# Transposing x by block loads and VectorE in place of TensorE, in a two-layer graph kernel

## The chip, the core and the metric

The kernel runs on one core of a Trainium2 chip. The core has a matrix engine (TensorE, PE in the profile), a vector engine (VectorE, DVE), a scalar engine (ScalarE, ACT), a general one (GpSimd, POOL) and a queue (SyncE, SP) that issues transfers to 16 DMA engines. Each engine works through its own queue in order; semaphores hold an instruction until what it needs is there. The metric is the time of one execution on the device in microseconds, as a median of several runs. All data is float32.

## The reference

x has 64 batches of 256 tokens with 512 features; `adj` is one 256 x 256 matrix of zeros and ones. Two layers follow each other, each with its input added and a layer norm after it:

```python
# layer 0: attention with 8 heads of 64, masked by adj
q, k, v = (x @ W + b for W, b in ((Wq, bq), (Wk, bk), (Wv, bv)))   # each 256 x 512 per batch
scores = q_h @ k_h.T / 8 + (1 - adj) * -1e9                         # per head
x = layernorm(x + (softmax(scores) @ v) @ Wo + bo)
# layer 1: graph attention with one pair of vectors a1, a2
h = x @ W
e = leaky_relu(s1[:, None] + s2[None, :], 0.2) * adj                # s1 = h @ a1, s2 = h @ a2
x = layernorm(x + elu(softmax(e) @ h + beta * h))
```

What matters here is `q`, `k` and `v`: TensorE sums over the partitions, so x must stand with its features on the partitions (x transposed, `xT`) before it can be multiplied by the weights. In memory it stands with tokens as rows.

## The kernel before

Work goes by pairs of batches. A pair has two halves, batch 0 and batch 1. The function `pair` makes `xT`, `qT`, `kT` and `V` for both; the function `batch` does the rest for each: scores and exponentials by keys (`scores`), their sums (`sums`) and reciprocals, the mix with V (`mix`), the output projection (`o`), the layer norm, the second layer's row and column terms (`logits`), its softmax and transpose (`attention`), its mix with x (`spread`), and the product with W (`u`), ending in `finish`.

`q`, `k`, `v`, `o`, `spread` and `u` are each done by `project` with seven block products in place of eight (Strassen's way, in Winograd's form), called `chain`, `cross`, `second`, `fourth` (or `pair`) after the PSUM tiles that they add into. The sums that this asks of the right side are made by GpSimd in `token_sums` (L393 to L412): `xS` from `xT`, `oS` from `oT`, `yS` from `yT`. The weights and sums of Wq and Wk are fetched anew for every pair, seven `piece` loads each (L386, L381), with six buffers.

Nothing is issued at once. `Plan.op` records an operation with its engine, an assumed duration, what it reads and what it writes; `Plan.place` then sets one order for all engines. TensorE's order is fixed by hand: `turn` gives each operation a pair (round, place in the round). `ROUND` (L23) is the order of the 20 stages in a round and `LATER` (L26) says how many rounds after the pair's number a stage runs, so that several pairs are in flight. Round r does `scores` and `v` of pair r, `q` and `k` of pair r + 1, `sums1` of pair r - 1, and so on. The other engines are filled around TensorE's order by due time, with limited buffers (`slots`); only TensorE's last 60 operations are placed by what is ready. The order that comes out is issued as it stands, so each engine's queue is fixed when the kernel is built. All transfers but a few at the start go through the one SP queue.

Around the change: x comes in twice. The second load (L673) is the residual, with tokens on the partitions. The first one (L600) feeds the transpose: four loads of 256 KB per pair into two buffers `xin`, whose rows are 2 KB each. TensorE transposes 128 x 128 blocks against an identity matrix into a PSUM tile `tr_x` (L593), four blocks per operation, 16 per pair, and ScalarE copies each PSUM tile into `xT` (L596). In a round the stage `x` stands behind `spread0` and is done for the next pair, which uses it in the same round at `q`.

Also near the change: after `sums`, VectorE takes the reciprocal `inv` (L741), SP stores it as `rows` (L752) and loads it back spread over partitions as `inv_all` (L756); VectorE then scales `oT` by it (L782), GpSimd makes `oS`, and `o` can run.

Of the kernel before, what the change touches and what calls it, by code (L numbers as in the profile page):

```python
# [16 lines left out]
P = 128  # L17
# [2 lines left out]
ALPHA = 0.2  # L20
NEG = -1000000000.0

ROUND = ("sums1", "mix1", "scores0", "v", "o1", "attention0", "u0", "spread0", "x", "logits1",  # L23
         "sums0", "mix0", "scores1", "q", "attention1", "o0", "spread1", "k", "logits0", "u1")

LATER = {"x": -1, "q": -1, "k": -1, "v": 0, "scores0": 0, "scores1": 0, "sums0": 0, "sums1": 1, "mix0": 0, "mix1": 1,  # L26
         "o0": 0, "o1": 1, "logits0": 0, "logits1": 1, "attention0": 1, "attention1": 1, "spread0": 1, "spread1": 1,
         "u0": 2, "u1": 1}
SAFE = 1e15


# [22 lines left out]
class Plan:  # L54
# [11 lines left out]
    SWITCH = 250.0  # L66
    LATER = 15000.0
    OPEN = 60
# [43 lines left out]
    def place(self):  # L112
# [21 lines left out]
        for n, o in enumerate(ops):  # L134
            if due[n] is None:
                due[n] = max((due[d] + (self.LATER if ops[d][0] == "PE" else ops[d][1]) for d in o[3]), default=0.0)

# [90 lines left out]
def gnn_two_layers(ctx: ExitStack, tc: tile.TileContext, x, adj, Wq, bq, Wk, bk, Wv, bv, Wo, bo, W, a, beta, out):  # L228
    nc = tc.nc
    B, N, D = x.shape  # L230
    NT = N // P
    C = D // P
# [6 lines left out]
    dram = ctx.enter_context(tc.tile_pool(name="dram", bufs=1, space=bass.MemoryType.DRAM))  # L239
# [14 lines left out]
    plan = Plan(slots)  # L254
    stay = []
    A = slice(None)

    def sb(tag, shape, name):
        return Buf(sb_pool, tag, [P] + shape, name)

    def ps(shape, name):
        return Buf(ps_pool, "ps", [P] + shape, name)
# [11 lines left out]
    def blk(t):  # L274
        return slice(t * P, (t + 1) * P)

    def half(i):
        return slice(i * F, (i + 1) * F)


    ident = const.tile([P, P], F32, name="ident")
# [4 lines left out]
    def load(w_sb, w):  # L286
        for c in range(C):
            plan.op("SP", 1000, lambda c=c: nc.sync.dma_start(w_sb[:, c], w[blk(c), :]), [], [(w_sb, c)])
# [40 lines left out]
    def transposed_mask():  # L329
        acc = ps([NT, N], "tr_adj")  # L330

        def pe():
            for k in range(NT):
                for t in range(NT):
                    nc.tensor.transpose(acc[:, k, blk(t)], adj_sb[:, t, blk(k)], ident)

        plan.op("PE", 430, pe, [adj_sb], [acc], claims=[maskT_sb])
        plan.op("DVE", 690, lambda: nc.vector.tensor_scalar(
            maskT_sb[A], acc[A], -1.0, -NEG * HD ** 0.5, ALU.add, ALU.mult), [acc], [maskT_sb])
# [53 lines left out]
    def token_sums(T, keys, name, width=P):  # L393

        S = sb("xS" if width == P else "xP", [3, 2, width], name)
        q = {(k, j): (lambda k=k, j=j: T[:, 2 * k:2 * k + 2, j * width:(j + 1) * width])
             for k in range(2) for j in range(2)}  # L400
        t2, t3, t4 = ((lambda i=i: S[:, i]) for i in range(3))

        def sub(dst, p, m, reads, writes):
            plan.op("POOL", 180 + 545 * width // P, lambda: nc.gpsimd.tensor_tensor(dst(), p(), m(), ALU.subtract),  # L404
                    reads, writes)

        sub(t3, q[1, 1], q[0, 1], keys(1, 1) + keys(0, 1), [(S, 1)])
        sub(q[0, 1], q[0, 1], q[0, 0], keys(0, 1) + keys(0, 0), keys(0, 1))
        sub(t2, q[1, 1], q[0, 1], keys(1, 1) + keys(0, 1), [(S, 0)])
        sub(t4, q[1, 0], t2, keys(1, 0) + [(S, 0)], [(S, 2)])  # L410
        return [(q[0, 0], keys(0, 0)), (q[1, 0], keys(1, 0)), (q[1, 1], keys(1, 1)), (t4, [(S, 2)]),
                (q[0, 1], keys(0, 1)), (t2, [(S, 0)]), (t3, [(S, 1)])]  # L412
# [51 lines left out]
    def gather(quarter, bias=None, wide=False):  # L464

        def copy(q, acc):
            (dst, key), (src, acc) = quarter(q), acc[::-1]
            if bias is None:
                plan.op("ACT", 590 if wide else 370, lambda: nc.scalar.copy(dst(), src()), [acc], [key])  # L469
                return  # L470
            for f in range(2):
                plan.op("ACT", 370, lambda f=f: nc.scalar.activation(
                    dst()[:, f, :], src()[:, f, :], AF.Identity,
                    bias=bias[:, 2 * q[0] + f:2 * q[0] + f + 1]), [acc], [key])

        def add(q, acc):
            (dst, key), (src, acc) = quarter(q), acc[::-1]
            plan.op("DVE", 690 if wide else 420, lambda: nc.vector.tensor_add(dst(), src(), dst()), [acc, key], [key])

        return copy, add  # L480
# [89 lines left out]
    def pair(m, at, general=False):  # L570

        def turn(what):

            plan.turn = ((m or 0) + LATER[what], ROUND.index(what))

        def dram(ap, s):
            return ap[at].rearrange("o (t p) d -> p o t d", p=P)[:, s]

        Xs = [sb("xin", [NT, D], f"xin_{m}_{s}") for s in range(2)]

        def tokens(s, t):
            return [(Xs[s], (t, 0)), (Xs[s], (t, 1))]


        xT, qT, kT = (sb("two", [C, 2 * N], f"{n}_{m}") for n in ("xT", "qT", "kT"))
        V = sb("two", [2 * NT, D], f"v_{m}")

        def tr_x(s, t):
            X, tr = Xs[s], ps([C, P], "tr_x")

            def pe():
                for c in range(C):
                    nc.tensor.transpose(tr[:, c, :], X[:, t, c * P:(c + 1) * P], ident)  # L593

            plan.op("PE", 430, pe, tokens(s, t), [tr], claims=[xT])
            plan.op("ACT", 680, lambda: nc.scalar.copy(xT[:, :, blk(2 * t + s)], tr[A]), [tr], [(xT, (t, s))])  # L596

        for s in range(2):
            for t in range(NT):
                plan.op("SP", 1400, lambda s=s, t=t: nc.sync.dma_start(Xs[s][:, t, :], dram(x, s)[:, t, :]), [],  # L600
                        tokens(s, t), first=m == 0 and s == 0 and t == 0)
        turn("x")
        for s in range(2):
            for t in range(NT):
                tr_x(s, t)

        right = token_sums(xT, lambda k, j: [(xT, (j, s)) for s in range(2)], "xS", N)

        def qk(left, bias, dst):
            project(left, right, True, [dst], *gather(  # L610
                lambda q: (lambda: dst[:, 2 * q[0]:2 * q[0] + 2, q[1] * N:(q[1] + 1) * N], (dst, q)), bias, True),
                width=N, raw=m == 0)

        if m == 0:
            wq_sb, wk_sb = sb("two", [C, D], "wq_sb"), sb("two", [C, D], "wk_sb")
            load(wq_sb, Wq)
            load(wk_sb, Wk)
            lq, left["q"] = streamed(wq_sb, Wq, "wq_sums")
            lk, left["k"] = streamed(wk_sb, Wk, "wk_sums")
            turn("q")  # L620
            qk(lq, bq_sb, qT)
            plan.turn = (plan.turn[0], plan.turn[1] + 0.5)
            transposed_mask()
            turn("k")
            qk(lk, bk_sb, kT)
            left["v"] = weight_sums(wv_sb, "sv_sb", "POOL")
            plan.turn = (0, ROUND.index("x"))
            left["o"] = residual_bias()
        else:
            turn("q")  # L630
            qk(left["q"], bq_sb, qT)
            turn("k")
            qk(left["k"], bk_sb, kT)
        turn("v")
        project(left["v"], right, False, [V], *gather(
            lambda q: (lambda: V[:, 2 * q[1]:2 * q[1] + 2, half(q[0])], (V, q)), wide=True), width=N)
        for s in range(2):
            batch(m, s, qT, kT, V, dram, general)

    def batch(m, s, qT, kT, V, dram, general):  # L640
# [5 lines left out]
        def turn(what):  # L646
            plan.turn = ((m or 0) + LATER[f"{what}{s}"], ROUND.index(f"{what}{s}"))

# [226 lines left out]
        if b == 0:  # L875
            plan.turn = (0, ROUND.index("k"))
            left["w"] = second_layer_constants()
# [123 lines left out]
    for m in range(B // 2):  # L1001
        pair(m, slice(2 * m, 2 * m + 2))
# [6 lines left out]
    def check():  # L1009
# [5 lines left out]
            claims=[least])  # L1015
# [9 lines left out]
    with tc.If(again != 0):  # L1025
# [3 lines left out]
        with tc.For_i(0, B, 2) as i:  # L1029
            for tile_ in stay:  # L1030
                tile_.parts = {}
            plan = Plan({**slots, "half": slots["half"] - 1})
# [33 lines left out]
```

## Time and profile before

| what | value |
|---|---|
| time, median of 3 runs (lowest to highest) | 2830.74 us (2830.37 to 2831.67) |
| span of the profiled execution | 2826.7 us |
| granted TensorE clock, mean | 0.997 |
| PE `tr_x`, L593 | 512 transposes, 63.1 us busy |
| ACT `xT`, L596 | 128 copies, 592 ns each in the median |
| loads of `xin`, L600 | 128 of 256 KB, 3.6 us from issue to landing |
| GpSimd `xS`, L404, idle ahead of it for ScalarE's `xT` | 87.8 us in 32 waits |
| HBM read and written | 220.73 MB and 36.17 MB |

How to read the profile: "busy" is the time in which an engine worked on an instruction; its share is of the span. PEld is TensorE's loading of the stationary operand, which runs beside its products. The chain of work that ended last is followed back from the last instruction, at each step to what released it, or to the instruction ahead of it on its engine. A group of instructions is a source line, an engine and the tiles written and read; "idle before" is time in which that engine had nothing to do just ahead of such an instruction, with the cause of most of it. One round is 86.75 us in the middle of the run.

### The profile page before, as it was taken

Reading aid. Unit: us, or ns where it says so; the run is one execution under the profiler, and the core shown is the slowest. Engines: PE = TensorE matmul, PEld = TensorE weight load, DVE = VectorE, ACT = ScalarE, POOL = GpSimd, SP = SyncE. Lnnn points to the kernel's source line nnn. Section 1 sums busy time; section 2 is a strip of 40 time slices with the busy share of each in tenths; the row PEclk is TensorE's granted clock in tenths of the full one; section 3 lists DMA queues with packets and bytes.
Section 4 is the critical chain, followed back from the end, with each engine's and each line's share of the span. In section 5 each row is a group of like instructions: output and inputs, shape, how many; then the busy total and the mean of one; then the engine's idle time right before and its main releaser. Section 6 shows DMA issues by size and latency. Waiting matters only on the chain.

```text
span 2826.7 us, 47456 instructions
## 1 busy us (share of the span) xinstructions
PE 2793.3 (99%) x16771; PEld 2367.1 (84%) x16771; DVE 2136.6 (76%) x4126; ACT 1319.3 (47%) x2875; POOL 1753.7 (62%) x2379
## 2 busy tenths in 40 slices
PE   9999999999999999999999999999999999999997
PEld 7788888888888888888888888888888888888875
DVE  6668777787877777777877777777778777787877
ACT  3345444454554444444544544445445444454544
POOL 5656765566655667556666556675566765566655
PEclk9999999999999999999999999999999999999999
DMA  6223322232222333323322223333233322232211
GB/s 231 75 75 106 98 86 76 86 113 90 91 91 79 101 98 98 94 67 95 113 90 87 81 81 113 90 98 95 71 98 105 97 87 75 87 112 90 75 44 41
DMA packets 181506, 260.07 MB, mean 92 GB/s; under 512 B 15256, under 2 KB 96400, under 8 KB 181264
## 3 DMA queue, kind: packets, MB, share of 16 engines
q1 hardware_dynamic: 181136, 256.95, 29.5%
q8 instruction: 137, 2.24, 0.3%
q14 instruction: 105, 0.86, 0.1%
q0 software_dynamic: 128, 0.01, 0.0%
HBM read 220.73 MB, written 36.17 MB: 91 GB/s over the span
## 4 chain that ended last, share of the span: by engine, by line
PE 97%; DVE 1%; POOL 0%; DMA 0%; ACT 0%; issue 0%; SPq 0%; DVEq 0%; POOLq 0%; ACTq 0%
PE ps_chain L433 32%; PE ps_cross L433 21%; PE ps_pair L433 10%; PE ps_sc L714 8%; PE ps_pv L691 8%; PE ps_fourth L433 6%; PE ps_second L433 6%; PE ps_den L737 2%; PE tr_x L593 2%; PE tr_a L929 1%; DVE junk L883 1%; PE tr_s L893 0%; PE ps_plain L497 0%; DVE junk L538 0%; DMA xin<-in_x_dram 0%
## 5 line engine op out<-in xcount | busy, mean ns | idle before, releaser
L725 POOL TENSOR_TENSOR both<-pT 128x256 f32<-128x256 f32 x512 | 368.5, 748 | 82.0 <-ACT pT L723 82.0
L723 ACT ACTIVATE pT<-pT 128x512 f32<-128x512 f32 x512 | 308.0, 630 | 123.2 <-DVE pT L721 122.0
L721 DVE TENSOR_TENSOR pT<-ps_sc,maskT_sb 128x512 f32<-128x512 f32 x512 | 316.2, 677 | 3.4 <-PE ps_sc L714 3.4
L883 DVE SCALAR_TENSOR_TENSOR junk<-x,wa_sb 128x512 f32<-128x512 f32 x256 | 246.4, 1015 | 0.7 <-ACT x L566 0.7
L714 PE MATMUL ps_sc<-qT,kT 64*128 64x256 f32 x2048 | 241.7, 384 | 2.6 <-DVE pT L721 2.6
L691 PE MATMUL ps_pv<-pT,v 128*64 128x256 f32 x2048 | 236.6, 384 | 0.0
L714 PEld LDWEIGHTS ps_sc<-qT,kT 64*128 64x128 f32 x2048 | 199.6, 187 | 43.6 <-issue 24.2
L560 POOL TENSOR_SCALAR rs<-mv 128x1 f32<-128x1 f32 x256 | 55.7, 218 | 286.5 <-DVE mv L557 284.2
L566 ACT ACTIVATE x<-x,nmr,rs 128x512 f32<-128x512 f32 x256 | 200.6, 811 | 48.3 <-DVE nmr L564 45.2
L911 POOL TENSOR_TENSOR e<-e,adj_sb 128x512 f32<-128x512 f32 (+1 forms) x65 | 91.5, 1408 | 205.9 <-DVE e L908 205.9
L691 PEld LDWEIGHTS ps_pv<-pT,v 128*64 128x64 f32 x2048 | 142.1, 137 | 91.8 <-issue 15.4
L969 POOL TENSOR_TENSOR att_sums<-attT 128x128 f32<-128x128 f32 x126 | 57.7, 458 | 203.0 <-ACT attT L933 191.7
L933 ACT COPY attT<-tr_a 128x512 f32<-128x512 f32 x64 | 37.5, 586 | 277.7 <-PE tr_a L929 277.6
L556 DVE BATCH_NORM_STATS2 bn<-x 128x6 f32<-128x512 f32 x256 | 164.5, 683 | 2.3
L675 POOL TENSOR_TENSOR x<-x,res_sb 128x512 f32<-128x512 f32 x128 | 161.0, 1279 | 2.2 <-issue 1.1
L561 POOL TENSOR_TENSOR rs<-rs,neg_half 128x1 f32<-128x1 f32 x256 | 145.4, 568 | 21.3
L564 DVE SCALAR_TENSOR_TENSOR nmr<-mv,rs 128x1 f32<-128x1 f32 x256 | 102.0, 408 | 72.5 <-POOL rs L561 72.1
L469 ACT COPY yT<-ps_chain 128x256 f32<-128x256 f32 x126 | 46.9, 373 | 231.4 <-PE ps_chain L433 225.2
L404 POOL TENSOR_TENSOR xS<-xT 128x512 f32<-128x512 f32 x64 | 87.4, 1366 | 90.3 <-ACT xT L596 87.8
L860 DVE TENSOR_TENSOR x<-x,ps_chain 128x256 f32<-128x256 f32 x252 | 100.2, 418 | 56.6 <-PE ps_chain L433 56.2
L969 POOL TENSOR_TENSOR X_sums<-x 128x256 f32<-128x256 f32 x126 | 120.4, 956 | 33.7 <-ACT x L566 33.7
L404 POOL TENSOR_TENSOR oS<-oT 128x256 f32<-128x256 f32 x126 | 92.5, 734 | 64.1 <-DVE oT L782 59.2
(232 smaller groups left out, 7482.9 us busy)
## 6 DMA issues: line engine op xcount, KB each, us to landing
xin<-in_x_dram SPq DMA_DIRECT2D x128, 256.0 KB, 3.6
x<-in_x_dram SPq DMA_DIRECT2D x64, 512.0 KB, 3.7
out_dram<-x SPq DMA_DIRECT2D x128, 256.0 KB, 3.1
inv_all<-rows SPq DMA_DIRECT2D x126, 256.0 KB, 3.8
wq_sums<-wq_sums SPq DMA_DIRECT2D x124, 256.0 KB, 2.6
wk_sums<-wk_sums SPq DMA_DIRECT2D x124, 256.0 KB, 2.8
wq_sums<-in_L_gnn_Wq_dram SPq DMA_DIRECT2D x93, 256.0 KB, 2.7
wk_sums<-in_L_gnn_Wk_dram SPq DMA_DIRECT2D x93, 256.0 KB, 2.8
```

The lines of the kernel that those rows point to most:

```text
L404: plan.op("POOL", 180 + 545 * width // P, lambda: nc.gpsimd.tensor_tensor(dst(), p(), m(), ALU.subtract), reads, writes)
L433: nc.tensor.matmul(dst[:, f, :], lhs, rhs, start=start and f == 0 and c == 0, stop=c == inner - 1, skip_group_check=True)
L556: plan.op("DVE", 690, lambda: nc.vector.bn_stats(bn[A], X[:, t, :]), [(X, (t, 0)), (X, (t, 1))], [bn])
L566: plan.op("ACT", 810, lambda: nc.scalar.activation(X[:, t, :], X[:, t, :], AF.Identity, bias=nm[A], scale=rs[A]), [nm, rs], [(X, (t, 0)), ...
L675: plan.op("POOL", 1270, lambda t=t: nc.gpsimd.tensor_tensor(X[:, t, :], X[:, t, :], res_sb[A], ALU.add), [res_sb], tokens(t))
L691: nc.tensor.matmul(acc[r * HD:(r + 1) * HD, i, :], V[:, 2 * k + s, h * HD:(h + 1) * HD], pT[h][:, k, :], start=k == 0, stop=k == NT - 1)
L714: nc.tensor.matmul(acc[j][:, k, :], kT[r:r + HD, c, key_blk(k)], own(qT, r, c), start=True, stop=True)
L721: plan.op("DVE", 690, lambda h=h, i=i: nc.vector.tensor_add(pT[h][A], acc[i][A], maskT_sb[A]), [acc[i], maskT_sb], [pT[h]])
L723: plan.op("ACT", 620, lambda h=h: nc.scalar.activation(pT[h][A], pT[h][A], AF.Exp, scale=1.0 / HD ** 0.5), [pT[h]], [pT[h]])
L725: plan.op("POOL", 725, lambda h=h, i=i: nc.gpsimd.tensor_tensor(both[c][:, i, :], pT[h][:, 0, :], pT[h][:, 1, :], ALU.add), [pT[h]], [(bot ...
L883: plan.op("DVE", 780, lambda t=t, i=i, junk=junk: nc.vector.scalar_tensor_tensor(junk[A], X[:, t, :], 1.0, wa_sb[:, i, :], op0=ALU.mult, o ...
L969: plan.op("POOL", ns, lambda: nc.gpsimd.tensor_tensor(dst(), p(), m(), op), reads, writes)
```

## The change

TensorE no longer transposes x. Each batch is loaded by four transfers, one for each group of 32 partitions `f`. A transfer puts 32 tokens on 32 partitions, and along each partition it lays runs of 32 features (128 bytes): partition `32 f + j` holds, for feature chunk `c` and token block `b`, the 32 features of token `32 b + j`. In that form every block of 32 tokens by 32 features lies on the right partitions and in the right columns, and only has to be transposed in itself. One VectorE instruction per batch does that for all 128 blocks and writes `xT` directly; PSUM and ScalarE are not used. An empty TensorE operation of the plan keeps the stage `x` a place in TensorE's order, which is where the buffer of `xT` is claimed.

The order of a round changes as well. `x` is done two rounds ahead in place of one (`LATER` -2), `u0` moves a round earlier and `u1` a round later, and `logits1`, `spread0`, `spread1`, `attention1`, `u0` and `u1` change places. The purpose is to take the transposes and their copies off TensorE and ScalarE, and to leave the loads and the transposes time ahead of `q`.

```diff
-ROUND = ("sums1", "mix1", "scores0", "v", "o1", "attention0", "u0", "spread0", "x", "logits1",
-         "sums0", "mix0", "scores1", "q", "attention1", "o0", "spread1", "k", "logits0", "u1")
+ROUND = ("sums1", "mix1", "scores0", "v", "o1", "attention0", "u1", "x", "spread0", "sums0", "mix0", "scores1", "q",
+         "logits1", "o0", "u0", "attention1", "k", "spread1", "logits0")
...
-LATER = {"x": -1, "q": -1, "k": -1, "v": 0, "scores0": 0, "scores1": 0, "sums0": 0, "sums1": 1, "mix0": 0, "mix1": 1,
+LATER = {"x": -2, "q": -1, "k": -1, "v": 0, "scores0": 0, "scores1": 0, "sums0": 0, "sums1": 1, "mix0": 0, "mix1": 1,
...
-         "u0": 2, "u1": 1}
+         "u0": 1, "u1": 2}
...
-        def tr_x(s, t):
-            X, tr = Xs[s], ps([C, P], "tr_x")
-
-            def pe():
-                for c in range(C):
-                    nc.tensor.transpose(tr[:, c, :], X[:, t, c * P:(c + 1) * P], ident)
-
-            plan.op("PE", 430, pe, tokens(s, t), [tr], claims=[xT])
-            plan.op("ACT", 680, lambda: nc.scalar.copy(xT[:, :, blk(2 * t + s)], tr[A]), [tr], [(xT, (t, s))])
-
+        def blocks(s):
+
+            xb = sb("xin", [C, N], f"xin_{m}_{s}")
+            rows = x[at].rearrange("o (b j) (c f i) -> o f j c b i", j=32, f=4, i=32)[s]
+            for f in range(4):
+                plan.op("SP", 700, lambda f=f: nc.sync.dma_start(
+                    xb[f * 32:(f + 1) * 32].rearrange("p c (b i) -> p c b i", i=32), rows[f]), [], [(xb, f)],
+                    first=m == 0 and s == 0 and f == 0)
+            plan.op("DVE", 1140, lambda: nc.vector.transpose(
+                xT[A].rearrange("p c (t s n) -> p c t s n", t=NT, s=2)[:, :, :, s, :],
+                xb[A].rearrange("p c (t n) -> p c t n", t=NT)), [xb, (xT, "turn")], [(xT, (t, s)) for t in range(NT)])
+
+
+        turn("x")
+        plan.op("PE", 0, lambda: None, [], [(xT, "turn")], claims=[xT])
         for s in range(2):
-            for t in range(NT):
-                plan.op("SP", 1400, lambda s=s, t=t: nc.sync.dma_start(Xs[s][:, t, :], dram(x, s)[:, t, :]), [],
-                        tokens(s, t), first=m == 0 and s == 0 and t == 0)
-        turn("x")
-        for s in range(2):
-            for t in range(NT):
-                tr_x(s, t)
+            blocks(s)
```

More of the change, by code (lines that the diff above doesn't have):

```diff
@@ L577, in dram @@
             return ap[at].rearrange("o (t p) d -> p o t d", p=P)[:, s]
-        Xs = [sb("xin", [NT, D], f"xin_{m}_{s}") for s in range(2)]
-        def tokens(s, t):
-            return [(Xs[s], (t, 0)), (Xs[s], (t, 1))]
         xT, qT, kT = (sb("two", [C, 2 * N], f"{n}_{m}") for n in ("xT", "qT", "kT"))
         V = sb("two", [2 * NT, D], f"v_{m}")
-        def tr_x(s, t):
-            X, tr = Xs[s], ps([C, P], "tr_x")
-            def pe():
-                for c in range(C):
-                    nc.tensor.transpose(tr[:, c, :], X[:, t, c * P:(c + 1) * P], ident)
-            plan.op("PE", 430, pe, tokens(s, t), [tr], claims=[xT])
-            plan.op("ACT", 680, lambda: nc.scalar.copy(xT[:, :, blk(2 * t + s)], tr[A]), [tr], [(xT, (t, s))])
-        for s in range(2):
-            for t in range(NT):
-                plan.op("SP", 1400, lambda s=s, t=t: nc.sync.dma_start(Xs[s][:, t, :], dram(x, s)[:, t, :]), [],
-                        tokens(s, t), first=m == 0 and s == 0 and t == 0)
-        turn("x")
-        for s in range(2):
-            for t in range(NT):
-                tr_x(s, t)
+        def blocks(s):
[10 more added lines that the diff above has]
+        plan.op("PE", 0, lambda: None, [], [(xT, "turn")], claims=[xT])
+        for s in range(2):
+            blocks(s)
         right = token_sums(xT, lambda k, j: [(xT, (j, s)) for s in range(2)], "xS", N)
```

## The prediction

> **What bounds the kernel now.** I read the page first: busy shares, then the chain that ended last.
>
> ```profile
> span 2826.7 us, 47456 instructions
> PE 2793.3 (99%) x16771; PEld 2367.1 (84%) x16771; DVE 2136.6 (76%) x4126; ACT 1319.3 (47%) x2875; POOL 1753.7 (62%) x2379
> PE 97%; DVE 1%; POOL 0%; DMA 0%; ACT 0%; issue 0%; SPq 0%; DVEq 0%; POOLq 0%; ACTq 0%
> ```
>
> PE is busy for 99% of the span and is 97% of the chain. A busy PE need not be a full one, so the next view is the table by stretches, for one round (two batches) in the middle, beside the first and the last stretch (columns: stretch, length, busy PE, PEld, DVE, ACT, POOL, clock, DMA share, GB/s).
>
> ```profile
> 0.00:88.00 88.00, 81.16 (x433) 68.04 (x434) 53.63 (x83) 31.41 (x64) 54.76 (x63) 1.00 0.61 204
> 1290.00:1376.75 86.75, 86.75 (x526) 73.82 (x525) 66.24 (x129) 41.25 (x90) 54.40 (x75) 1.00 0.30 92
> 2740.00:2827.00 87.00, 64.80 (x343) 49.62 (x339) 68.18 (x152) 35.67 (x75) 46.45 (x70) 0.92 0.14 47
> ```
>
> A round in the middle has no idle PE at all: 86.75 of 86.75 us, at full clock. So its length is the sum of what stands in PE's queue, and a matmul removed there shortens it by its place in the queue, as long as no wait opens. VectorE has 20.5 us free in a round, ScalarE 45, GpSimd 32, and the DMA engines 70%. How much the transposes hold is read in the timeline of PE (start, length, line, names), from their start to the next group's:
>
> ```profile
> 1346.89 0.61 PE L433 MATMUL ps_chain<-att_sums,X_sums 128*128 128x128 f32 x4
> 1347.34 1.91 PE L593 MATMUL tr_x<-ident,xin 128*128 128x128 f32 x16
> 1349.09 0.38 PE L893 MATMUL tr_s<-ident,s 128*128 128x128 f32 x2
> ```
>
> 16 transposes hold PE from 1347.34 to 1349.09: 1.75 us, 109 ns each, though one lasts 272 ns by itself (they overlap). Last, the chain at the start, where x is wanted at once:
>
> ```profile
> 1.67 4.34 DMA xin<-in_x_dram
> 6.05 1.98 PE tr_x L593 x8
> 8.05 0.59 ACT xT L596
> 8.72 1.28 POOL xS L404
> ...
> 14.13 1.99 PE ps_fourth L433 x8
> ```
>
> Here the load of x stands on the path, then ScalarE's copy, then four GpSimd sums, and PE's `fourth` product waits for these.
>
> **What the Trainium skill says.** "TensorE: Matmul & The Clock Gate", Part 4: PE-mode transpose, has about 275 ns for a transpose in a kernel's context; the trace agrees (272 ns), but back to back it is the 109 ns that count. "VectorE: DVE Perf Modes", The three transpose paths: VectorE transposes blocks of 32 by 32 alone, each on its own; so the loads have to put the blocks in their places, and no trace here shows it. "SBUF — State Buffer", Who interferes with whom: VectorE contends with GpSimd when it has two inputs in SBUF, not with one input outside the two-port modes. The trace agrees: a 128x512 addition with one input in PSUM takes 677 ns (L721), one with both in SBUF 994 ns (L782). A transpose has one input, so I take it as undisturbed. "DMA: Bandwidth & Descriptors", Specifications: line rate wants at least 512 bytes in a run. The change makes runs of 128 bytes; no load of this size of run is in the trace.
>
> **The change, part by part.**
>
> (1) *Removed from PE*: 32 groups of 1.75 us. One stands in the start, which I cost by itself; 31 x 1.75 = **54.3 us** off the path, in rounds with no idle PE.
>
> (2) *Removed from ScalarE*: 128 copies of 598 ns, 76.5 us. ScalarE is 47% busy and is not on the chain: 0 us. Four PSUM banks per pair come free: 0 us.
>
> (3) *Added to VectorE*: 64 transposes of 128x1024. Skill ("Vector Engine (DVE) Microarchitecture Reference", The reshape front-end and per-opcode configuration): one element per cycle per lane. From the trace: a 128x512 sum takes 687 ns (L478) and a 128x256 one 418 (L860), so 1.05 ns per element and 0.15 us fixed; for 1024 elements 1.2 us. Lower end 1.1 (no fixed part), upper end 2.3 (half rate). I take 1.2: 2.4 us in a round, VectorE at 68.6 of 85.0 us, hidden beside PE's products. In the built order the first transpose of a round stands among the yT sums of the `spread` stage, the second among the qT sums, and x is made more than a round ahead of `q`. Behind the first wait the yT sums (for GpSimd's yS and then `u`), behind the second the qT sums (for the next scores). But the loads of a buffer are issued right after the transpose that empties it, a round (85 us) before the next one, so the data has landed: no wait, and some 1.2 us of delay in a queue with 16 us to spare.
>
> (4) *The loads*: 128 of 256 KB in rows of 2 KB become 256 of 128 KB in runs of 128 bytes: 512 runs per pair and DMA engine in place of 32 rows. The price p of a run is the disputed number. In the trace's records of single packets a 2048-byte one takes 84 ns (median), a 1024-byte one 46; the line through both has 8 ns fixed and 128 bytes at **13 ns** (low end). If each costs as a 512-byte run: 8 + 19 = **27 ns**. As a 1024-byte packet: **46 ns** (high end). I take **20**, between the first two. Per round: 10.2 us of each DMA engine in place of 2.7, so the DMA share rises from 0.30 to about 0.40: no bound.
>
> (5) *What is queued behind the loads.* All loads go through one SP queue. In the built order the loads of one batch stand just ahead of the `rows`/`inv_all` pair that `o0` needs. That batch's 4 x 64 runs take 256 x p: 3.3, 5.1, 6.9 or 11.8 us at p = 13, 20, 27, 46. `rows` is issued some 5 us after its sums start (1349.40 to 1354.93 in the round above), the loads about 0.5 us after; so `rows` starts late by 0, 0.5, 2 or 7 us. Slack: GpSimd ended `oS` at 1368.2, `o0` began at 1370.37 and uses `oS` 2.6 us later, so 4.8 us; the new order brings `o0` 1.3 us nearer (no transposes between), so 3.4. Delay below that: 0 us. At 46 ns it costs 3.4 us in each of 31 rounds.
>
> (6) *The start.* Loads begin at 1.67; eight take 512 x p; completion adds 1.65 (4.34 less 32 x 84 ns), the last transpose 1.2. xT is there at 11.2, 14.8, 18.3 or 28.1 us in place of 8.65: +2.5, **+6**, +9.6, +19.4. The second pair's loads follow 17 weight loads of 0.67 us each, and VectorE's transposes of them stand ahead of the last kT sums, on which the first scores wait: no stall at 20 ns, 1.6 us at 27, 11.4 at 46.
>
> (7) *The order of a round.* `logits1`, `u0`, `u1`, `attention1`, `spread1` change places; PE's sum stays 85.0 us. Most distances grow (`o1` to `logits1` from 11 to 30 us, `spread1` to `u1` from 12 to 33). One shrinks: `logits1` to `attention1` from 20.5 to 12.1 us (`o0` and `u0` between). That chain's rows sum to 6.6 us (L902 twice 0.47, L908 0.69, L911 1.43, L913 0.68, L916 twice 0.50, L919 0.17, L922 twice 0.83), which leaves 5.5 us for queueing behind eight x sums of 0.42 and two statistics of 0.68: just enough, 0 us. The end has the same products to do after the last scores: 0, give or take 4.
>
> Sum: 2830.7 - 54.3 + 6 = **2782 us**.
>
> **The rivals.**
>
> A, the forecast: everything hidden but the start. p of 13 gives 2779, 27 gives 2788. For it: no idle PE, VectorE at 76%. Chance 0.70.
>
> B, another wait takes part of it: the short `logits1` to `attention1` path, or a transpose standing in VectorE's queue ahead of scores that PE wants. For it: z began 5.5 us after its row was there in the round above, so VectorE does queue. Against: the chain has 5.5 us to spare. At 1 us a round, 2782 + 31 = 2813. Chance 0.12.
>
> C, the short runs are dear (46 ns): 2830.7 - 54.3 + 30.8 (start) + 31 x 3.4 = 2913, slower than before. For it: no run of 128 bytes is priced in the trace and the skill warns of them. Against: the DMA engines are 70% idle and packet times follow the bytes down to 1 KB. Something between, that cancels the gain, is 0.03. C has 0.15.
>
> **How the numbers follow.** Predicted: A's 2782. The range reaches from 2774 (cheap runs, an end that is 4 us better) to 2826 (B at 1.4 us a round); it leaves out C, the case that cancels, and a sliver below. Faster: A and B, 0.82; same 0.03; slower 0.15.
>
> **What would show it.** Right: a middle round of 85.0 us with no idle PE; no PE row at the transposes' line and no `xT` copy on ScalarE; VectorE transposes near 1.2 us with no idle time ahead of them in the middle; PE's first product some 6 us later. Wrong at (4) and (5): DMA share over 0.45 in a middle round, PE idle ahead of `ps_chain<-wo_sb,oT` or `ps_chain<-so_sb,oS`. Wrong at (3): transposes of 2 us or more. Wrong at (7): PE idle ahead of `tr_a`, released by VectorE.

## The result, and the profile after

The changed kernel takes 2782.23 us in the median of four runs (2781.12 to 2782.5), the kernel before, run beside it, 2830.66 us (2830.37 to 2831.67). The ratio is 0.9828, with a 95% interval of 0.9811 to 0.9845: faster by 48.4 us. The forecast was 2782.

First the page of the kernel after: span, busy time of each engine with its share and instructions, and the shares of the chain that ended last.

```profile
span 2780.4 us, 46736 instructions
PE 2738.3 (98%) x16259; PEld 2312.2 (83%) x16259; DVE 2067.6 (74%) x4190; ACT 1238.7 (45%) x2747; POOL 1759.1 (63%) x2379
PE 97%; DVE 2%; issue 0%; SPq 0%; POOL 0%; DMA 0%; ACT 0%; POOLq 0%; DVEq 0%; ACTq 0%
```

PE's busy time fell by 55.0 us (2793.3 to 2738.3) and its idle time rose by 8.7 (span less busy: 33.4 to 42.1), which makes the 46.3 us between the two spans. Where the idle time lies is read in the table by stretches of the kernel after (stretch, length, busy PE, PEld, DVE, ACT, POOL, granted share of TensorE's full clock, DMA share, GB/s):

```profile
0.00:88.00 88.00, 69.17 (x352) 57.30 (x353) 58.40 (x75) 25.02 (x51) 48.41 (x55) 0.96 0.75 199
1290.00:1375.00 85.00, 85.00 (x511) 72.02 (x510) 63.55 (x130) 38.65 (x86) 54.64 (x74) 1.00 0.35 94
2692.00:2780.00 88.00, 66.52 (x335) 51.67 (x333) 64.58 (x150) 34.17 (x74) 42.33 (x67) 0.88 0.14 46
```

A round in the middle is 85.0 us of PE without a gap. In the first stretch PE's idle time went from 6.8 us to 18.8; over the first 175 us together from 11.4 to 20.1, since the second stretch of 87 us has a little less (4.6 before, 1.3 after). That is all of the 8.7; the last stretch has 21.5 against 22.2, and from 175 to 2692 us PE's gaps add up to 0.1 us. VectorE is the surprise: 78.8 us of transposes came in, and it is busy for 69 us less than before.

The new row, from the groups of instructions (busy and mean ns, then idle time of VectorE just ahead of it):

```profile
L591 DVE STREAM_TRANSPOSE xT<-xin 128x1024 f32<-128x1024 f32 x64 | 78.8, 1232 | 2.5 <-DMA xin<-in_x_dram 2.2 <-issue 0.3
```

That is 1.23 us a transpose, and no wait but a single one at the start. The chain of the first 25 us (start, length, what) of the kernel after:

```profile
6.24 1.20 SPq L588
...
7.49 3.55 DMA xin<-in_x_dram
...
11.16 1.26 DVE xT L591
...
12.46 3.78 PE ps_chain L433 x8
16.24 2.70 PE ps_second L433 x8
18.94 1.73 PE ps_fourth L433 x8
```

SP issues eight loads one behind the other, from 0.74 to 7.44 us (L588 is the load), then comes the rest of the transfer, then the second transpose. The first product starts at 12.46 in place of 7.84 us, `fourth` at 18.94 in place of 14.13. The first two products are also slower: from the first one's start to the end of the second 6.5 us, for 5.2 before.

### The profile page after: what moved, and what is told of

Its sections match the earlier page's. It is cut to its first block, busy times and chain, and to the rows that moved or that the text cites. A ratio compares the mean times of both kernels' runs of the same rounds, so it can differ in the third digit from the quotient of the medians.

```text
span 2780.4 us, 46736 instructions
## 1 busy us (share of the span) xinstructions
PE 2738.3 (98%) x16259; PEld 2312.2 (83%) x16259; DVE 2067.6 (74%) x4190; ACT 1238.7 (45%) x2747; POOL 1759.1 (63%) x2379
## 4 chain that ended last, share of the span: by engine, by line
PE 97%; DVE 2%; issue 0%; SPq 0%; POOL 0%; DMA 0%; ACT 0%; POOLq 0%; DVEq 0%; ACTq 0%
PE ps_chain L433 33%; PE ps_cross L433 22%; PE ps_pair L433 10%; PE ps_sc L708 8%; PE ps_pv L685 8%; PE ps_second L433 6%; PE ps_fourth L433 6%; PE ps_den L731 2%; PE tr_a L923 1%; PE tr_s L887 0%; DVE junk L877 0%; SPq L588 0%; PE ps_y L938 0%; DVE x L650 0%; PE ps_plain L497 0%
## 5 line engine op out<-in xcount | busy, mean ns | idle before, releaser
L717 ACT ACTIVATE pT<-pT 128x512 f32<-128x512 f32 x512 | 296.5, 625 | 113.6 <-DVE pT L715 113.4
L560 POOL TENSOR_SCALAR rs<-mv 128x1 f32<-128x1 f32 x256 | 62.7, 245 | 351.7 <-DVE mv L557 342.8
L877 DVE SCALAR_TENSOR_TENSOR junk<-x,wa_sb 128x512 f32<-128x512 f32 x256 | 195.4, 800 | 0.0
L404 POOL TENSOR_TENSOR yS<-yT 128x256 f32<-128x256 f32 x126 | 103.4, 820 | 144.1 <-DVE yT L478 139.1
L910 ACT ACTIVATE e<-e,nm 128x256 f32<-128x256 f32 x128 | 64.7, 506 | 255.5 <-DVE nm L907 255.5
L561 POOL TENSOR_TENSOR rs<-rs,neg_half 128x1 f32<-128x1 f32 x256 | 155.3, 607 | 21.3
L963 POOL TENSOR_TENSOR X_sums<-x 128x256 f32<-128x256 f32 x126 | 107.1, 850 | 66.4 <-ACT x L566 66.4
L905 POOL TENSOR_TENSOR e<-e,adj_sb 128x512 f32<-128x512 f32 (+1 forms) x65 | 82.1, 1263 | 85.5 <-DVE e L902 84.1
L771 ACT COPY oT<-ps_pv 128x512 f32<-128x512 f32 x128 | 75.1, 586 | 131.8 <-PE ps_pv L685 129.6
L433 PE MATMUL ps_chain<-sw_sb,yS 128*128 128x256 f32 x504 | 129.3, 379 | 0.0
```

Of the source, the lines that this page charges most:

```text
L433: nc.tensor.matmul(dst[:, f, :], lhs, rhs, start=start and f == 0 and c == 0, stop=c == inner - 1, skip_group_check=True)
L561: nc.gpsimd.tensor_tensor(rs[A], rs[A], neg_half, ALU.pow)
L717: plan.op("ACT", 620, lambda h=h: nc.scalar.activation(pT[h][A], pT[h][A], AF.Exp, scale=1.0 / HD ** 0.5), [pT[h]], [pT[h]])
L877: plan.op("DVE", 780, lambda t=t, i=i, junk=junk: nc.vector.scalar_tensor_tensor(junk[A], X[:, t, :], 1.0, wa_sb[:, i, :], op0=ALU.mult, o ...
```

## The experiments

A ratio is against the kernel before, run in the same set. The kernel after, at 2782.2, was run in another set, and the runs of one kernel lie 1 to 7 us apart; so a difference of 1 or 2 us from it is no more than that spread. All the edits go through the planner again, which places the queues of VectorE, ScalarE and GpSimd anew.

### What the order is worth

**The order alone.** The kernel before with the new `ROUND` and `LATER`; x still by whole rows, TensorE and ScalarE.

> The kernel before with the changed round order alone (ROUND and LATER of the change; x still loaded in whole rows and transposed by TensorE, ACT copies kept). Theory: the whole gain is TensorE's 54 us of transposes; the order is worth nothing by itself, since TensorE never idled in a middle round: 2826 to 2836 us, TensorE busy 2793 us. Rival 1: the order carries part of the gain (fewer stalls at the ends or less contention): under 2815 us. Rival 2: the order costs something with the old transposes, which the change pays for: over 2840 us. A side question: VectorE's busy time fell from 2136.6 to 2067.6 us although 78.8 us of transposes came in; if the order does this, VectorE's busy time here is about 1990 us, if not it stays at 2136.

Measured: 2832.22 us, ratio 1.0007 (0.9999 to 1.0015). The order by itself gives nothing, as the theory had it. PE's idle time in the first 175 us is 11.4 us, the same as before, so the 8.7 us more of the kernel after come with the loads and the transposes. The side question is answered too: VectorE's busy time is 2051.6 us, 85 less than before with the same instructions. The rows with two inputs in SBUF are shorter: L883 848 ns in the mean for 1015, L922 613 for 830; one is longer, L656 1033 for 691. So it is the order that freed VectorE (the expectation of 1990 took the transposes off as well, which was too simple).

**The blocks alone.** The changed kernel with the old `ROUND` and `LATER`.

> The changed kernel with the round order of before (blocks and VectorE transposes, old ROUND and LATER). Theory: the gain is TensorE's time, so nearly all of it stays, and the order only gives the loads and the softmax chain more room: 2780 to 2795 us. Rival (the prediction's case B): without the order the x chain, or logits1 to attention1 shortened by the missing transposes, becomes a wait in each round of 1 to 2.5 us: 2810 to 2860 us, with TensorE idle before its product on xT or before the transposes of the softmax's a.

Measured: 3018.24 us, ratio 1.0658 (1.0644 to 1.0673): 188 us slower than before, outside the theory's 2780 to 2795 and even the rival's 2810 to 2860. PE was idle for 183.5 us of the span of 3020.5. PE's waits over the whole run (us in total, times, longest), and then PE's and VectorE's timelines in one round of this kernel:

```profile
PE tr_a L923 <- DVE e L916: 83.7, 58, 2.5
PE ps_sc L708 <- DVE inv L735: 25.4, 29, 0.9
PE ps_cross L433 <- POOL attT L963: 23.3, 31, 1.0
```

```profile
1377.14 0.30 PE L923 MATMUL tr_a<-ident,e 128*128 128x128 f32 x1 [2.48 <-DVE e L916]
1377.91 0.88 PE L923 MATMUL tr_a<-ident,e 128*128 128x128 f32 x3 [0.48 <-DVE e L916]
1378.59 1.92 PE L433 MATMUL ps_chain<-wo_sb,oT 128*128 128x256 f32 x4
```

```profile
1352.43 2.35 DVE L591 STREAM_TRANSPOSE xT<-xin 128x1024 f32<-128x1024 f32 x2
1354.71 2.33 DVE L650 SCALAR_TENSOR_TENSOR x<-u,x 128x512 f32<-128x512 f32 x2
1356.96 1.75 DVE L735 RECIPROCAL inv<-ps_den 128x256 f32<-128x256 f32 x1
```

The two transposes stand one behind the other in VectorE's queue, in the very stretch, from 1347.3 to 1374.0 us, in which it has no gap. The second layer's softmax (z, e, and the transposes `tr_a` of it) has to get through that queue. The last of the three PE lines shows a second loss: the four products behind the wait take 1.92 us, while the same group takes 1.03 us undisturbed. There the granted clock was down to half, as the first line below shows. But that doesn't follow every such wait: four rounds earlier (from the second line on) an equal wait has the same group behind it in 1.03 us.

```profile
1378.00:1381.40 3.40, 3.40 (x10) 2.86 (x11) 0.42 (x1) 0.58 (x1) 3.15 (x4) 0.50 0.22 86
...
1006.63 0.30 PE L923 MATMUL tr_a<-ident,e 128*128 128x128 f32 x1 [2.48 <-DVE e L916]
...
1007.79 1.03 PE L433 MATMUL ps_chain<-wo_sb,oT 128*128 128x256 f32 x4
```

Over the run PE's busy time is 2837.0 us against 2738.3 after, and the mean clock 0.978 against 0.995. Of the 240 us between the spans of this kernel and the one after, 141 are idle time and 99 are time booked as busy. The clock makes some 52 of the 99, by an estimate from the means and the spans: 0.022 x 3020.5 = 66 us lost here, 0.005 x 2780.4 = 14 after. The other 47 are not explained by it: a round at full clock (1102.30 to 1194.45) is also booked with 87.28 us of busy PE, for 85.0 after.

Something else differs besides the place of the transposes. With the same instructions VectorE is busy for 2247.9 us here and for 2067.6 after: the rows with two inputs in SBUF are longer, L877 1181 ns in the mean for 800. From the first of the four L877 rows (L883 in the kernel before) to the end of e is 30.6 us here and 26.1 before. The transposes make 2.35 of the 4.5 us; the longer L877 and L650 make about 2. No run parts the two.

Why was there so little room? The kernel before already lay near the edge there; VectorE's and then PE's timeline of before:

```profile
1367.58 1.81 DVE L922 SCALAR_TENSOR_TENSOR e<-e,rc,diag_sb 128x256 f32<-128x256 f32 x2
```

```profile
1369.94 0.60 PE L929 MATMUL tr_a<-ident,e 128*128 128x128 f32 x4
```

VectorE ended at 1369.39, PE began at 1369.94: 0.6 us to spare, though `logits1` (`tr_s` in PE's queue) had been done 20.5 us earlier. VectorE had been busy without a gap since 1343.3.

**ScalarE copies in place of the transposes, old order.** The transpose of the kernel above becomes:

```diff
-            plan.op("DVE", 1140, lambda: nc.vector.transpose(...), [xb, (xT, "turn")], [...])
+            for t in range(NT):
+                plan.op("ACT", 680, lambda t=t: nc.scalar.copy(xT[:, :, blk(2 * t + s)], xb[:, :, blk(t)]), ...)
```

> Block loads in the old round order, but ScalarE copies each block to xT where VectorE transposed it (four copies of 128x512 a pair, as many as before the change); xT then holds untransposed blocks, so later values differ and the work does not. It takes VectorE's 2.35 us a pair away and keeps TensorE's missing 1.75 us. Accounting theory: in the kernel before, TensorE's transposes of the softmax's a began only 0.6 us after VectorE's last scaling of e, with VectorE busy without a gap for 26 us ahead of it; the blocks alone take 1.75 us of TensorE's work out of that stretch and put 2.35 us of VectorE's in, 0.6 - 1.75 - 2.35 = -3.5 us a round. Without VectorE's part, 0.6 - 1.75 = -1.15 us a round and a slower clock after each wait: 2810 to 2870 us. If VectorE's added time alone makes the 3018 us: 2775 to 2790. If only the lost TensorE time (the shorter way from logits1 to attention1) makes it: 2980 or more.

Measured: 2935.53 us, ratio 1.0371 (1.0353 to 1.0388), in none of the three ranges. `tr_a` still waited for VectorE's e, 77.9 us in 58 waits for 83.7. VectorE's queue shows why the account failed: e begins 14.5 us behind z (1307.28 to 1321.80), with other work between them without a gap, where the kernel above had 11.2 us. With other durations the planner fills a queue in another way, so taking one item out doesn't shift the rest by its length. The account also left out that rows change their length: L877 has a mean of 1192 ns, for 1015 of the same row before. So the transposes on VectorE are a part of the loss; the sum "0.6 - 1.75 - 2.35" isn't shown.

**x a round early, old order.** `x` alone goes to its new place, ahead of `spread0`, with `LATER` -2.

> Blocks and VectorE's transposes in the old round order, but x alone moved to where the new order has it (a round earlier, ahead of spread0). Accounting theory: the two transposes leave the full stretch of VectorE ahead of the softmax, the shorter TensorE way stays: 2810 to 2870 us, like ScalarE copies in their place. If x's place is all that the new order is worth: 2778 to 2795. If it is worth nothing and the place of logits1 and attention1 does it all: 3000 or more.

Measured: 2849.61 us, ratio 1.0059 (1.0042 to 1.0076), in the range of the theory. The place of x (its round and its place in it) is worth 169 of the 236 us by which the times of the old and the new order differ; the other 67 are of the rest. The waits of `tr_a` for e fall from 83.7 to 2.9 us; in their place PE waits for VectorE's pT ahead of `ps_sc` (19.2 us in 30 waits). Between the spans of this kernel and the one after, 30 us are idle time and 38 are booked as busy, at a mean clock of 0.994 for 0.995: the clock isn't the reason here, and which one it is stays open.

**x a round late, new order.** `LATER["x"]` is -1 in place of -2, nothing else.

> The changed kernel with x at the same place of the new round order but a round later (offset -1 for -2), so that loads and transposes come due only a few products ahead of q. Theory: what counts is which stretch of VectorE's queue holds the transposes, and the stretch after scores1 has room: 2780 to 2800 us. Rival: a round of distance is needed, since the loads land late or VectorE is behind: TensorE waits for xT, 2820 us or more.

Measured: 2837.39 us, ratio 1.0021 (1.0014 to 1.0027). The 55 us are more than the whole gain of the change, and the time is the rival's; but its reason isn't. PE never waited for xT in the middle. From the timelines of VectorE and PE of this kernel:

```profile
1350.83 2.37 DVE L591 STREAM_TRANSPOSE xT<-xin 128x1024 f32<-128x1024 f32 x2
```

```profile
1363.76 1.99 PE L433 MATMUL ps_chain<-xT,wq_sums 128*128 128x256 f32 x8 [1.73 <-DVE pT L715]
```

Without the round in hand the planner puts both transposes together, ahead of `inv` and of the masked exponents pT, into VectorE's full stretch; PE then stands for 1.73 us in each round. That is nearly all of the loss (the waits for pT add up to 50.5 us from 200 to 2700 us): PE's busy time is 2739.7 us, as after, and the clock from 300 to 2700 us stays at 1.00, so these waits have no slower products behind them. `ps_chain` doesn't read pT; what it must be waiting for, by the kernel's eight PSUM buffers, is a tile that the additions of pT have yet to read out. With the round in hand it sets one at 1325.93 and the other at 1343.04, into places with less behind them. So the early x buys freedom to place, not time for the loads to land. A part of the delay isn't the transposes' own, though: the two L650 rows between them and pT take 2.86 us here and 1.35 after, and this was not separated.

**logits1 in its old place, new order.**

```diff
-... "x", "spread0", "sums0", "mix0", "scores1", "q", "logits1", "o0", ...
+... "x", "spread0", "logits1", "sums0", "mix0", "scores1", "q", "o0", ...
```

> The changed kernel with logits1 alone moved back to its old place, right behind x and spread0 and ahead of sums0 and scores1 (x, u0 and u1 as changed). The old order with x early still lost 67 us, with VectorE busy without a gap ahead of scores1 and its masked exponents pT late. Theory: that rest is logits1's place, whose four products of 0.7 to 1.2 us on VectorE, behind the updates of u, fall into the stretch ahead of scores1's pT: 2815 to 2850 us, with waits of TensorE for VectorE's pT or e. Rival: the places of u0 and u1 are the rest, and logits1 may stand where it will: 2780 to 2795.

Measured: 2800.18 us, ratio 0.9892 (0.9876 to 0.9909), between the two ranges. logits1's place is worth 18 us, with PE waiting for pT again (0.45 us idle in each middle round). It doesn't make up the 67; whether the places of `u0`, `u1`, `attention1` and `spread1` are the rest was not tried and stays open.

### What the loads and the transposes cost

**Each transpose twice**, from the third pair on:

```diff
+            for _ in range(1 if m is None or m < 2 else 2):
                 plan.op("DVE", 1140, lambda: nc.vector.transpose(
```

> The changed kernel with each VectorE transpose done twice from the third pair on (2.4 us more VectorE work a pair, 30 pairs). Theory: there is room in the new order where they stand (2.7 us of idle VectorE after the second of a round), only the first can delay the reciprocal of the softmax sums behind it by up to 0.8 us: 2782 to 2807 us. Rival (case B of the prediction, VectorE near its bound): 2.4 us a round and more with the slower clock, 2850 to 2920 us.

Measured: 2784.93 us, ratio 0.9834 (0.9818 to 0.985). 2.3 us more of VectorE in each round, and PE still has no gap in the middle (table by stretches of this kernel):

```profile
1290.00:1375.00 85.00, 85.00 (x511) 72.03 (x511) 65.86 (x133) 38.69 (x87) 54.54 (x74) 1.00 0.35 94
```

The 2.7 us lie in the first 175 us, where PE's idle time is 22.4 for 20.1. The same transposes that are ruinous in the old order are all but free in the new one, even doubled.

**Seven eighths of each block load twice**, from the third pair on, into a tile that nobody reads:

```diff
+                if m is not None and m > 1:
+                    plan.op("SP", 700, lambda f=f: nc.sync.dma_start(
+                        spare[...].rearrange("p c (b i) -> p c b i", i=32), rows[f][:, :, :7]), [], [(xb, f)])
```

> The changed kernel, where from the third pair on seven eighths of each x block is loaded a second time, in the same 128-byte runs and on the same queue, into a tile that nobody reads (one buffer of the 18 half-size ones given up for it). Theory: the loads are off the path; 57,000 x 4 more... in sum 215,000 more packets of 13 ns over 16 engines are 0.175 ms of the span, so a DMA share of about 0.41 for 0.35 in a middle round, which stays 85.0 us: 2781 to 2788 us in all. Rival (case C of the prediction in another size: the issues and runs ahead of the rows and inv_all of o0 on the queue use up their slack of 3.4 us): 1 to 5 us a round, 2813 to 2940 us.

Measured: 2782.29 us, ratio 0.9826 (0.9813 to 0.9839). Its middle round, and the line of its queue (packets, MB, share of 16 engines):

```profile
1290.00:1375.00 85.00, 85.00 (x516) 72.04 (x512) 63.57 (x131) 38.54 (x86) 54.58 (x75) 1.00 0.41 105
```

```profile
q1 hardware_dynamic: 647824, 284.50, 40.3%
```

218,882 more packets, 40.3% of the engines' time for 34.0%: at 13 ns each they are 178 us on each of 16 engines, 6.4% of the span. PE has no wait for these loads, and the middle round no gap. Rival C is out, with nearly twice the short runs.

**The same loads as rows of 2 KB.**

```diff
-                    xb[f * 32:(f + 1) * 32].rearrange("p c (b i) -> p c b i", i=32), rows[f]), ...
+                    xb[f * 32:(f + 1) * 32].rearrange("p (g c) n -> p g (c n)", g=2),
+                    x[at][s].rearrange("(g f p) d -> f p g d", g=2, f=4)[f]), ...
```

> The changed kernel with the same four loads of 128 KB for a batch element and the same VectorE transposes, but each load moves rows of 2 KB (two per partition) instead of 128-byte runs; x then lies at other places, so q, k and v are of permuted data (the values of the output differ, the work does not). Theory: 128-byte runs cost 13 ns each and are hidden in all middle rounds, so only the start gains (issue time and transfer): a middle round stays 85.0 us, the total 2773 to 2781. Rival (case C): short runs hold back the rows and outputs behind them on the queue in each round: 2750 to 2770.

Measured: 2780.74 us, ratio 0.9824 (0.981 to 0.9837): 1.5 us below after, in the theory's range, but no more than the spread. The middle round is 85.0 us with no gap, as with the short runs, so these cost nothing there. What they cost at the start this run can't tell. The first product comes at 11.7 for 12.5 us, but PE's idle time in the first 175 us is 20.1 us in both. And the start has another limit now, as VectorE's timeline shows:

```profile
8.90 0.48 DVE L532 TENSOR_SCALAR diag_sb<-ident,beta_sb 128x128 f32<-128x128 f32 x2 [8.90 <-DMA beta_sb<-in_L_gnn_beta_dram]
9.30 2.37 DVE L592 STREAM_TRANSPOSE xT<-xin 128x1024 f32<-128x1024 f32 x2
```

Ahead of the transposes in VectorE's queue stands `diag_sb`, a constant of the second layer, and waits until 8.9 us for the load of `beta_sb`. Both transposes follow one behind the other. In the kernel after `diag_sb` runs at 7.3 us, and the second transpose waits for its load.

### The start

**The first pair on TensorE**, by whole rows as before; the other 31 pairs by blocks.

> The changed kernel, but the first pair's x is loaded in whole rows and transposed by TensorE as before; the other 31 pairs as changed. Theory: the block loads' issue time at the start (eight of 0.7 to 1.5 us) costs the start 8 to 10 us, and the old start costs 1.75 us of TensorE instead: 2772 to 2777 us, with the first product at about 8.7 us and TensorE idle in the first 175 us about 12 us instead of 20. Rival: the later stall at 65 us only grows by what the start gives up, and the total stays within 1.5 us of 2782.

Measured: 2778.36 us (2776.49 to 2779.1), ratio 0.9813 (0.98 to 0.9827). The gain is 3.9 us of the 5 to 10 expected: PE's idle time in the first 175 us falls from 20.1 to 13.3 us, but 1.75 us of transposes come back and the second stall stays.

**Two queues.** The first pair's loads with odd `f` are issued by ScalarE.

> The changed kernel, with every second block load of the first pair issued from ScalarE's queue instead of SyncE's; all else as changed. Theory: the late first product (xT at 12.5 us) comes of eight issues of 0.7 to 1.5 us one behind the other, 7.4 us; two queues halve that: first product 3 us earlier, 2778 to 2780 us. Rival: the transfer itself (3.5 us behind the last issue) or the descriptors' handling is what takes the time, whichever queue issues: within 1 us of 2782.

Measured: 2780.88 us, ratio 0.9825 (0.9811 to 0.9838): 1.4 us below after, less than the theory's 2 to 4 and within the spread; PE's idle time in the first 175 us is 19.1 us for 20.1. The chain of its start, and VectorE's timeline:

```profile
3.51 6.07 DMA xin<-in_x_dram
...
10.22 1.21 DVE xT L592
...
11.48 3.78 PE ps_chain L433 x8
```

```profile
8.66 0.48 DVE L532 TENSOR_SCALAR diag_sb<-ident,beta_sb 128x128 f32<-128x128 f32 x2 [8.66 <-DMA beta_sb<-in_L_gnn_beta_dram]
9.06 2.37 DVE L592 STREAM_TRANSPOSE xT<-xin 128x1024 f32<-128x1024 f32 x2
```

All eight loads are issued by 4.95 us, 2.5 earlier than in the kernel after, but the one that lands last comes only 1.5 earlier (9.58 for 11.04). So the issues are not the whole of it. The runs themselves are the next limit, by an estimate: 512 runs of 13 ns are 6.7 us of each DMA engine, most of the time between the first issues, done at 1.5 us, and the landing. Of the 1.5 us, 0.5 are lost again on VectorE, where `diag_sb` waits until 8.66 us and holds back the first transpose, and so the second.

**The constants later.** In the kernel after PE stalls a second time, from 65 to 71.5 us, as PE's waits show:

```profile
PE ps_chain L433 <- DVE pT L715: 6.4, 1, 6.4
```

Seven of eight products of W and a (L538, up to 1.75 us each) stand ahead of the additions of pT in VectorE's queue. With the first pair on TensorE, these products are made to wait for the first batch's `oT`:

```diff
-                    [w_sb, a_sb], [junk, (col, c)])
+                    [w_sb, a_sb] + after, [junk, (col, c)])
...
-            left["w"] = second_layer_constants()
+            left["w"] = second_layer_constants([(oT, 0)])
```

> The changed kernel with two edits: the first pair's x in whole rows and transposed by TensorE (2778.4 us by itself), and the eight products of W and a on VectorE (second_layer_constants) made to wait for the first batch's oT, so that they no longer stand ahead of the first pair's masked exponents pT in VectorE's queue. Theory: TensorE's second stall, 6.2 us at 61 to 67 us <- VectorE pT, and the slow clock behind it go: 2770 to 2774 us. Rival: the eight products then hold up VectorE's additions to q and the logits of the first batch, and the stall only moves: 2776 to 2780 us.

Measured: 2775.14 us (2772.51 to 2775.74), ratio 0.9804 (0.979 to 0.9817). It lies between the two ranges: the stall (6.2 us with the first pair on TensorE alone) is gone, one of 2.1 us opens where VectorE's additions to x now come behind those products. This is the fastest version, 7.1 us below the kernel after. The gain lies in the first 88 us, where PE is idle for 8.0 us in place of 18.8.

## Why the prediction was right, point by point

**(1) TensorE: held.** 54.3 us were forecast; PE's busy time fell by 55.0, and in the middle rounds no idle time took their place.

**(2) ScalarE: held.** Busy 80.6 us less, nothing moved by it.

**(3) The transposes: right size, right outcome, wrong argument.** 1.2 us forecast, 1.23 measured, no waits. But "16 us to spare" in a round was the reason given, and it doesn't carry: in the old order VectorE had as much to spare on average, and the same transposes came with 188 us of loss. What hides them is where they stand, and what the order makes of the rows around them: the step took their places from the built order, but didn't say that the round order is the reason why they can stand there. The forecast of 68.6 us of VectorE in a round was too high (63.6); by the order alone VectorE's two-input rows get shorter, and the step had left these at their old lengths. On these rows the Trainium skill ("SBUF — State Buffer", Who interferes with whom) says that VectorE contends with GpSimd when both inputs are in SBUF. The same row at 848 and 1015 ns in two orders fits that, though how much of the difference GpSimd makes was not measured.

**(4) The price of a run: at its low end.** 20 ns taken, 13 measured in the records of single packets, as the line through the two packets of before had it. The middle round's DMA share is 0.35, not the 0.40 of the step.

**(5) The queue: held.** `inv_all` is issued 2.17 us behind `rows` for 1.77, and the doubled loads show that there was room for more.

**(6) The start: the sum came out, its terms didn't.** At the forecast's 20 ns the step gives xT at 14.8 us, at the measured 13 ns at 11.2. It came at 12.4, late by 3.8 in place of 2.5 us against before. The term that was missing is the issue of the loads: the step let the transfer begin at 1.67 and run at the price of its packets alone, while SP's issue of a block load takes 0.67 us in the median for 0.42 of a whole-row one, and each transpose has to wait for four loads of its batch. The too dear p covered that. The first products were slower, and PE's second stall, 1.6 us in before, became 6.4, which the step didn't have; the new order alone has it at 6.1. The small stalls of before, of 0.8 and 1.9 us near 131 us, went in exchange. All in all the total is 5.9 us above 2830.7 - 54.3, where 6 were forecast, and that so exact a sum is right is luck in part: a run too dear stood in for issues and a stall left out.

**(7) The order: held, and undervalued.** `logits1` to `attention1` is 12.3 us apart as forecast, "just enough". First PE's, then VectorE's timeline of the kernel after:

```profile
1347.67 0.38 PE L887 MATMUL tr_s<-ident,s 128*128 128x128 f32 x2
...
1359.97 0.60 PE L923 MATMUL tr_a<-ident,e 128*128 128x128 f32 x4
```

```profile
1356.37 0.88 DVE L916 SCALAR_TENSOR_TENSOR e<-e,rc,diag_sb 128x256 f32<-128x256 f32 x2
```

VectorE ends at 1357.25, 2.7 us ahead of PE, though the way is 8.5 us shorter than before, where it had 0.6. The 0 us for the order is right for the order alone (+1.8 us measured). As part of the change it decides the sign: without it, 3018.

**The rivals.** B did not happen, but it was near: the old order, x a round later, or logits1 in its old place each bring it about, with 18 to 236 us. In the old order it would have ended well outside the case that was worked out (1 us a round): each round there has several waits, 4.6 us of idle PE in all, with the clock at half behind some of them. C is excluded.

## What to carry to other kernels

Free time on an engine is a property of a stretch, not of a round: before work is put on an engine that is 76% busy, look in its timeline for the runs without a gap, and for what the bounding engine fetches from their ends. Work that needs an input long before its use should be allowed to run early, because a scheduler can then put it where nothing waits behind it; here one number in `LATER` is worth 55 us, more than the whole change brought. And in a start with nothing to hide behind, work with a part of the load is better than a wait for all of it: the first pair by whole rows, transposed as they land, was worth 3.9 us here.

## What the runs showed of the hardware

- A run of 128 bytes takes 13 ns of a DMA engine, beside 46 for 1024 bytes and 84 for 2048: some 10 bytes per ns in place of 24, and no step upward at this size.
- Behind a wait of TensorE of 2.5 us and one of 0.5 the granted clock was half for 3.4 us in one round (a group of 1.03 us took 1.92) and full in another (1.03). Waits of 1.73 us, one in each round, left it at 1.00.
- VectorE rows with two inputs in SBUF have no fixed price: the same 256 rows of 128x512 took 800 ns in the mean in one order and 1181 in another. The transposes, with one input, took 1.19 to 1.25 us in every order tried.
- VectorE transposes 32 x 32 blocks of a 128x1024 float32 tile in 1.23 us, about the 1.2 us estimated from its additions; for two such tiles TensorE was held for 1.75 us and ScalarE for 2.4 before.
